# Where a hand-paced attention loop may place the work that runs behind it

## The chip, the cores and the metric

The kernel runs on one core of one Trainium2 chip. The metric is the device time of one execution in microseconds. TensorE, VectorE, ScalarE, GpSimd and the SyncE queue (PE, DVE, ACT, POOL and SP in the profile) each work through their own instructions in order and wait for each other by semaphores; PEld is TensorE's loading of weights.

## The reference

The input is `x` of shape (8, 128, 36, 36), so 8 batch items of N = 1296 positions with 128 channels, in float32. Layer 0 is a convolution with attention; layer 1 is an additive attention over the positions, then a small mixture of experts. Nearly all the time goes to the additive attention, whose score is a sum over 128 channels for each pair of positions:

```python
q = jnp.einsum('bld,ed->ble', x, Wq) + bq
k = jnp.einsum('bld,ed->ble', x, Wk) + bk
t = jnp.tanh(q[:, :, None, :] + k[:, None, :, :])
scores = jnp.einsum('bijd,d->bij', t, w) + bw[0]
attn = jax.nn.softmax(scores, axis=-1)
return jnp.einsum('bij,bjd->bid', attn, x)
```

The kernel does not evaluate the tanh pair by pair. It writes tanh(q + k) as a quotient of sums of exponentials that separate into a part of the query and a part of the key. A matmul of query features `qf` and key features `kf` gives denominators `d`, a second one, with the weighted part of `qf`, gives numerators `n`, and the score is a sum of n/d over groups of channels.

## The kernel before, in words

**The loop.** There are 8 batches, 3 chunks of 432 queries and 11 key tiles, which makes 264 units of (batch, chunk, tile). A unit of a full key tile has 12 slots, k = 0 to 11; the tile with the 16 keys left over (a remainder unit) has 2. That makes 2928 slots, 366 in a batch. In slot p the loop issues, in this order (lines 1031 to 1058):

- `take_turns(p)`: steps of the work behind the loop that need no matmul, such as a VectorE or ScalarE operation that takes the result of a matmul out of PSUM (a "take");
- `numerators(p)` (L903): two matmuls into two banks `n`;
- `denominators(p + LAG)`, LAG = 3 (L886): two matmuls into two banks `d`, for the slot three ahead, and on ScalarE the logarithm of both banks into `lq` (L898) and, in every other slot, the exponential of minus that, four banks at once (L901), so that `lq` holds 1/d;
- `terms(p, ns)` (L908): VectorE multiplies `n` by 1/d;
- `matmul_turn(p)`: at most one group of matmuls of the work behind the loop, which stands on TensorE between d of this slot and n of the next.

**Shapes of the slots.** For k = 0, 1, 3, 4, 6, 7, 9, 10 each matmul contracts 32 rows, on one half of the rows, and n of slot p and d of slot p + 3 use opposite halves. For k = 2, 5, 8, 11 each contracts 64 rows (SLOTS, lines 48 to 53). A float32 matmul shows as two instructions.

**Who sums.** In the 8 slots of a unit that are not in `DVE_PAIRS`, VectorE writes two products to `rp` (L929, two operations) and GpSimd adds them up (L936, L938). In the 4 slots k = 2, 5, 8, 11, VectorE multiplies in place (L923) and adds both banks to `accd` itself (L925), so it has four operations there in place of two; for k = 2 there are three (L918 to L920). At the end of a unit GpSimd joins both sums (L945, L947), and ScalarE takes the exponential of the score (L958).

**Banks.** `ps_d` holds two slots' denominators. `ps_n` is a ring of four banks: two for the numerators of each slot, and each group of the work behind the loop takes one from the same ring. `lq` has three buffers, each for two slots.

**The work behind the loop.** Generators yield before each group of matmuls and before each take. They stand in four lanes (L991), asked in this order: `first_of_all` (features of the next queries, scores of the remainder), `urgent` (the weighted sum of the finished chunk, `attend`), `gates` (the gating of the batch before) and `background` (normalization, convolutions, layer 0, tokens and keys of the next batch). A lane's generator says whether it wants matmuls next and how many slots it rests first. Each group adds its columns, plus 20 per matmul, to `behind[0]` (L256); most groups count 148 to 904 such columns.

**The pace.** `balance` gains PACE columns in every slot and loses what was issued; lanes other than `first_of_all` may issue a group only if it is not negative, and it never rises above PACE. Once a group has been issued, `matmul_turn` stops for this slot:

```python
            before = behind[0]
            for lane in lanes:
                while lane.due(p, True) and behind[0] == before:
                    if lane is not first_of_all and balance[0] < 0 or lane is gates and urgent:
                        break
                    lane.run(p)
            balance[0] = min(balance[0] - (behind[0] - before) + PACE, PACE)
```

`take_turns` asks each lane once, in every slot. Key features go to DRAM and are loaded again two units ahead of their use (`prefetch`, SP's queue). Before the loop the first batch is prepared; after it the experts follow.

Of the kernel before, what the change touches and what calls it, by code (L numbers as in the profile page):

```python
# [55 lines left out]
LAG = 3  # L56
SHIFT = 6.5
DVE_PAIRS = (2, 5, 8, 11)
PACE = 365

# [7 lines left out]
def kernel(  # L70
# [55 lines left out]
    with ExitStack() as loop, ExitStack() as score:  # L126
# [127 lines left out]
        behind = [0]  # L254
# [128 lines left out]
        def conv_keys(b):  # L383
            k = convolved["k"] = big_tile("k0")
            for r0, nr in KROWS:
                yield from conv_turns(
                    taps["k"], (r0, nr), 1, grid(k[:, r0 * WV : (r0 + nr) * WV], WV), True
                )
# [246 lines left out]
        def keys(b, tiles):  # L635

            xT = prepared[b][1]
            yield matmuls(1)
            for t in tiles:
                o, n = KT[t]  # L640
                for q0 in (0, NF // 2):
                    some = slice(q0, q0 + NF // 2)
                    pk = aux("pk1").rearrange("p (q t) -> p q t", t=128)
                    for q in range(NF // 2):
                        bmm(pk[:, q, :n], a_k[:, (q0 + q) * 128 : (q0 + q + 1) * 128],
                           xT[:, o : o + n], start=True, stop=True)
                    yield TAKE
                    ks = kstp.tile([128, NF // 2, 128], F32, tag="ks", name="ks")
                    nc.scalar.activation(ks[:, :, :n], pk[:, :, :n], AF.Exp)
                    kd3 = kd[b][t].rearrange("p (q t) -> p q t", t=128)[:, some, :]  # L650
                    if n == REM:

                        for x in range(2):
                            nc.gpsimd.tensor_scalar(
                                ks[:, :, (x + 1) * n : (x + 2) * n], ks[:, :, :n],
                                pairs[:, min(q0, 1), x : x + 1], None, ALU.mult,
                            )
                        nc.sync.dma_start(kd3[:, :, : 2 * n], ks[:, :, n : 3 * n])
                    else:
                        nc.sync.dma_start(kd3, ks)  # L660
                    if q0 > 0:
                        made.add((b, t))
                    yield matmuls()
# [58 lines left out]
        def gating(b):  # L722
            yield from gate_logits(b, range(NCH))
            yield from gate_tokens(b)
# [122 lines left out]
        slots = []  # L847
# [4 lines left out]
        def prefetch(u):  # L852
            if u < len(units):
                b, c, j = units[u]
                assert (b, j) in made
                n = 128 if j < NKT - 1 else 32
                kf = kfp.tile([128, NF, 128], F32, tag="kf", name="kf")
                nc.sync.dma_start(
                    kf[:, :, :n], kd[b][j].rearrange("p (q t) -> p q t", t=128)[:, :, :n]
                )  # L860
                kf_of[u] = kf

        def new_block(b, c, q):
            qf = qfp.tile([128, 2, CH], F32, tag="qf", name="qf")
            qf_of[b, c, q] = qf
            return query_block(b, c, q, qf)
# [19 lines left out]
        def denominators(p):  # L886

            if p >= len(slots):
                return
            u, k = slots[p]  # L890
            d = ps_d.tile([128, 2, 512], F32, tag="d", name="d")
            n = banks(u, k)
            products(u, k, 0, [d[:, h, :] for h in range(n)])
            if k % 2 == 0:
                lq_of[u, k // 2] = lp.tile([128, 4, CH], F32, tag="lq", name="lq")
            lq = lq_of[u, k // 2]
            o = 2 * (k % 2)
            nc.scalar.activation(lq[:, o : o + n, :], d[:, :n, :CH], AF.Ln)  # L898
            if k % 2 == 1:
                some = lq[:, : o + n, :]  # L900
                nc.scalar.activation(some, some, AF.Exp, scale=-1.0)  # L901

        def numerators(p):  # L903
            ns = [ps_n.tile([128, 512], F32, tag="n", name="n") for _ in range(banks(*slots[p]))]
            products(*slots[p], 1, ns)
            return [ps[:, :CH] for ps in ns]

        def terms(p, ns):  # L908

            u, k = slots[p]  # L910
            lq = lq_of[u, k // 2]
            o = 2 * (k % 2)
            mult = nc.vector.tensor_mul
            rem = units[u][2] == NKT - 1
            if k in DVE_PAIRS and not rem:
                if k == DVE_PAIRS[0]:
                    live["d"] = acc.tile([128, CH], F32, tag="accd", name="accd")
                    mult(live["d"], ns[0], lq[:, o, :])  # L918
                    mult(ns[1], ns[1], lq[:, o + 1, :])
                    nc.vector.tensor_add(live["d"], ns[1], live["d"])  # L920
                else:
                    for h in range(2):
                        mult(ns[h], ns[h], lq[:, o + h, :])  # L923
                    for h in range(2):
                        nc.vector.tensor_add(live["d"], ns[h], live["d"])  # L925
            else:
                rp = rpp.tile([128, 2, CH], F32, tag="rp", name="rp")
                for h, n in enumerate(ns):
                    mult(rp[:, h, :], n, lq[:, o + h, :])  # L929
                if rem:  # L930
                    live.setdefault("rem", []).extend(rp[:, h, :] for h in range(len(ns)))
                elif k == 0:
                    live["r"] = rp
                elif k == 1:
                    live["p"] = acc.tile([128, 2, CH], F32, tag="accp", name="accp")
                    nc.gpsimd.tensor_add(live["p"], live["r"], rp)  # L936
                else:
                    nc.gpsimd.tensor_add(live["p"], live["p"], rp)  # L938
            if k % 2 == 1:
                lq_of.pop((u, k // 2))  # L940
# [50 lines left out]
        first_of_all, urgent, gates, background = lanes = [Lane() for _ in range(4)]  # L991
        balance = [0]

        def take_turns(p):
            for lane in lanes:
                if lane.due(p, False):
                    lane.run(p)

        def matmul_turn(p):


            before = behind[0]
            for lane in lanes:
                while lane.due(p, True) and behind[0] == before:
                    if lane is not first_of_all and balance[0] < 0 or lane is gates and urgent:
                        break
                    lane.run(p)
            balance[0] = min(balance[0] - (behind[0] - before) + PACE, PACE)

        load_x(1)  # L1010
        drain(normal(0))
# [15 lines left out]
        for p, (u, k) in enumerate(slots):  # L1027
            b, c, j = units[u]
            rem = j == NKT - 1
            if k == 0:  # L1030
                prefetch(u + 2)
                if c == 0 and j == 1:
                    if b > 0:
                        gates.append(gating(b - 1))
                    if b + 1 < NB:
                        background.extend(
                            (normal(b + 1), conv_keys(b + 1), layer0(b + 1), tokens(b + 1),
                             keys(b + 1, range(NKT)))
                        )
            take_turns(p)  # L1040
            ns = numerators(p)
            denominators(p + LAG)
            terms(p, ns)
            if pending and pending[0][0] <= p:
                exps(p, *pending.popleft()[1:])
            last = p + 1 == len(slots) or slots[p + 1][0] != u

            if j == order[-1] and u + 1 < len(units) and k % 3:
                used = IN_TURN.index(SLOTS[k][0]) + 1
                if used < NF:  # L1050
                    first_of_all.append(new_block(*units[u + 1][:2], IN_TURN[used]))
            elif j == order[-2] and last and u + 2 < len(units):
                first_of_all.append(new_block(*units[u + 2][:2], IN_TURN[0]))
            matmul_turn(p)
            if last and rem:
                first_of_all.append(rem_scores(p, u, live.pop("rem")))
            elif last:
                pending.append((p + 7, u, sums(u)))
        while pending:
            exps(p, *pending.popleft()[1:])  # L1060
        take_turns(len(slots))
        assert not first_of_all and not gates and not background
        score.close()

# [41 lines left out]
    gates, res = [], []  # L1106
# [140 lines left out]
```

## Time and profile before

| what | value |
|---|---|
| median of 3 runs | 6183.36 us (6181.84 to 6194.64) |
| the profiled execution | 6189.61 us |
| its span, first to last instruction | 6187.9 us |
| mean granted TensorE clock | 0.979 |
| start of batch 1, 3, 4 and 7 in the loop | 921.5, 2400.0, 3140.6, 5359.5 us |
| last slot starts | 6014.0 us |
| L898, logarithm of two banks on ScalarE | 2928 of 879 ns |
| L901, exponential of four banks on ScalarE | 1464 of 1638 ns |
| L929, L923, L925 on VectorE | 600, 608, 603 ns each |
| L938 on GpSimd | 1440 of 2024 ns |
| matmuls of n and of d, per instruction | 574 and 563 ns |

The profile lists instructions by line, engine and tile: `n<-qf,kf` is a matmul that writes numerators, `pa`, `s`, `pc`, `pk` and the like are banks of the work behind the loop. A wait is named as waiting engine and tile, then the one that released it, with the sum of time, how often, and the longest. Batches and slots are told apart in the timeline by counting the numerator matmuls: four instructions in each slot of a full tile.

### The profile page before, as it was taken

How to read it: one execution, taken by the hardware profiler on the slowest of the kernel's cores; microseconds unless marked ns; L12 is line 12 of the kernel's file. 1: busy time of each engine (PE TensorE's matmuls, PEld its weight loads, DVE VectorE, ACT ScalarE, POOL GpSimd, SP SyncE). 2: the span in 40 equal slices, each digit the busy share in tenths (PEclk: the TensorE clock that was granted, in tenths of full speed). 3: DMA queues.
4: the chain of work that ended last, by engine and by line, in shares of the span. 5: the costliest groups of instructions: out<-in, count | busy, mean ns of one | idle time of the engine just before them, and what ended most of it. 6: DMA issues, size and time to landing. Idle time of an engine off the chain costs nothing.

```text
span 6187.9 us, 93159 instructions
## 1 busy us (share of the span) xinstructions
PE 5946.4 (96%) x33576; PEld 2834.5 (46%) x33576; DVE 4799.7 (78%) x9525; ACT 5275.0 (85%) x5371; POOL 4584.2 (74%) x2794
## 2 busy tenths in 40 slices
PE   7999999999999999999999999999999999999996
PEld 5454444544544445444445444454444444544443
DVE  3687778877788787877887777887778878788872
ACT  1798998988989888889988899898998988999980
POOL 3677877777778777778777786877777777787870
PEclk9999999999999999999999999999999999999997
DMA  1210011000110002100111001110011000100017
GB/s 43 70 36 22 21 68 38 33 26 28 67 39 24 26 30 69 37 24 23 50 48 38 22 24 63 41 36 22 21 65 41 31 25 28 63 31 28 25 55 276
DMA packets 150383, 271.40 MB, mean 44 GB/s; under 512 B 45408, under 2 KB 74976, under 8 KB 149920
## 3 DMA queue, kind: packets, MB, share of 16 engines
q1 hardware_dynamic: 149920, 265.44, 12.8%
q8 instruction: 265, 4.34, 0.3%
q14 instruction: 198, 1.62, 0.1%
HBM read 200.94 MB, written 64.19 MB: 43 GB/s over the span
## 4 chain that ended last, share of the span: by engine, by line
PE 65%; DVE 11%; POOL 8%; ACT 8%; issue 8%; DMA 1%; SPq 0%; POOLq 0%; DVEq 0%; ACTq 0%
PE n L875 30%; PE d L875 10%; PE pa L258 7%; ACT lq L898 5%; PE pc L258 5%; DVE n L923 4%; POOL accp L938 4%; DVE rp L929 3%; PE s L258 3%; PE pk L258 3%; DVE accd L925 2%; POOL qf L673 1%; POOL accp L936 1%; PE d L880 1%; PE pq L258 1%
## 5 line engine op out<-in xcount | busy, mean ns | idle before, releaser
L938 POOL TENSOR_TENSOR accp<-accp,rp 128x864 f32<-128x864 f32 x1440 | 2915.1, 2024 | 996.5 <-DVE rp L929 943.5
L875 PE MATMUL n<-qf,kf 32*128 32x432 f32 (+1 forms) x11520 | 3283.6, 574 | 58.9 <-DVE accd L925 19.1
L898 ACT ACTIVATE lq<-d 128x864 f32<-128x864 f32 x2928 | 2517.6, 879 | 555.8 <-PE d L875 498.0
L875 PE MATMUL d<-qf,kf 32*128 32x432 f32 (+1 forms) x11520 | 2907.7, 563 | 46.4 <-ACT lq L898 40.5
L929 DVE TENSOR_TENSOR rp<-n,lq 128x432 f32<-128x432 f32 x3912 | 2160.8, 600 | 557.9 <-PE d L875 398.8
L901 ACT ACTIVATE lq<-lq 128x1728 f32<-128x1728 f32 (+1 forms) x1464 | 2398.2, 1638 | 46.3
L875 PEld LDWEIGHTS n<-qf,kf 32*128 32x128 f32 (+1 forms) x11520 | 1185.9, 185 | 1588.2 <-DVE rp L929 469.1
L875 PEld LDWEIGHTS d<-qf,kf 32*128 32x128 f32 (+1 forms) x11520 | 1046.9, 186 | 449.8 <-issue 241.7
L923 DVE TENSOR_TENSOR n<-n,lq 128x432 f32<-128x432 f32 x1440 | 812.0, 608 | 251.8 <-PE n L875 195.2
L925 DVE TENSOR_TENSOR accd<-n,accd 128x432 f32<-128x432 f32 x1440 | 868.1, 603 | 24.7
L936 POOL TENSOR_TENSOR accp<-rp 128x864 f32<-128x864 f32 x240 | 485.2, 2022 | 244.8 <-DVE rp L929 244.7
L673 POOL TENSOR_SCALAR qf<-qf,cs_s 128x432 f32<-128x432 f32 x192 | 260.7, 1364 | 47.0 <-ACT qf L672 47.0
L258 PEld LDWEIGHTS pa<-xh,e 128*108 128x108 f32 x1920 | 222.1, 174 | 142.9 <-DVE rp L929 63.3
L947 POOL TENSOR_TENSOR accd<-accp,accd 128x432 f32<-128x432 f32 x240 | 265.3, 1106 | 23.3 <-DVE accd L925 3.0
L258 PE MATMUL pa<-xh,e 128*108 128x129 f32 x1920 | 261.3, 283 | 19.9 <-DVE accd L925 13.9
L945 POOL TENSOR_TENSOR accp<-accp 128x432 f32<-128x432 f32 x240 | 264.7, 1103 | 15.8
L258 PE MATMUL s<-q,k 128*116 128x432 f32 x480 | 230.3, 568 | 4.2 <-DVE accd L925 2.7
L444 ACT ACTIVATE e<-s 116x432 f32<-116x432 f32 x240 | 124.8, 520 | 118.7 <-PE s L258 118.4
L258 PEld LDWEIGHTS pk<-xT,a_k 128*128 128x128 f32 x1408 | 171.6, 193 | 105.9 <-DVE n L923 31.8
L435 POOL TENSOR_TENSOR tot<-tot,e 116x432 f32<-116x432 f32 x192 | 212.1, 1105 | 7.3 <-ACT e L444 4.5
L918 DVE TENSOR_TENSOR accd<-n,lq 128x432 f32<-128x432 f32 x240 | 145.1, 604 | 86.7 <-PE n L875 49.7
L258 PE MATMUL pa<-e,vw 116*128 116x432 f32 x480 | 204.6, 549 | 0.0
(208 smaller groups left out, 3870.2 us busy)
## 6 DMA issues: line engine op xcount, KB each, us to landing
kf<-kd SPq DMA_DIRECT2D x240, 512.0 KB
kd<-ks SPq DMA_DIRECT2D x160, 256.0 KB
w<-in_weight_dram SPq DMA_DIRECT2D x32, 1024.0 KB
wk_t<-wk_t_d SPq DMA_DIRECT2D x7, 768.0 KB
wv_t<-wv_t_d SPq DMA_DIRECT2D x7, 768.0 KB
wq_t<-wq_t_d SPq DMA_DIRECT2D x7, 768.0 KB
x<-in_x_dram SPq DMA_DIRECT2D x8, 648.0 KB
t<-tokd SPq DMA_DIRECT2D x96, 54.0 KB
```

Source lines behind the costliest of these rows:

```text
L258: mm(out, lhsT, rhs, **kw)
L673: nc.gpsimd.tensor_scalar(qf[:, 1, :], qf[:, 0, :], cs_s[:, q : q + 1], None, ALU.mult)
L875: mm(outs[h][:, :CH], kf[rows[h], q, :], qf_of[b, c, q][rows[h], part, :], start=True, stop=True)
L898: nc.scalar.activation(lq[:, o : o + n, :], d[:, :n, :CH], AF.Ln)
L901: nc.scalar.activation(some, some, AF.Exp, scale=-1.0)
L923: mult(ns[h], ns[h], lq[:, o + h, :])
L925: nc.vector.tensor_add(live["d"], ns[h], live["d"])
L929: mult(rp[:, h, :], n, lq[:, o + h, :])
L936: nc.gpsimd.tensor_add(live["p"], live["r"], rp)
L938: nc.gpsimd.tensor_add(live["p"], live["p"], rp)
L945: nc.gpsimd.tensor_add(s[:, 0, :], s[:, 0, :], s[:, 1, :])
L947: nc.gpsimd.tensor_add(d, s[:, 0, :], d)
```

## The change

`take_turns` and `matmul_turn` are told k, the number of the slot in its unit. In slots k = 2, 5, 8, 11 `take_turns` now serves only the lane `first_of_all`. `matmul_turn` now lets the other three lanes issue no group if the next slot is one of these four. PACE rises from 365 to 400 columns, and what is saved up may reach 800 in place of 365. The call after the loop passes k = 0.

```diff
-PACE = 365
+PACE = 400
...
-        def take_turns(p):
+        def take_turns(p, k):
             for lane in lanes:
-                if lane.due(p, False):
+                if lane.due(p, False) and (k not in DVE_PAIRS or lane is first_of_all):
                     lane.run(p)
 
-        def matmul_turn(p):
+        def matmul_turn(p, k):
...
             before = behind[0]
             for lane in lanes:
                 while lane.due(p, True) and behind[0] == before:
-                    if lane is not first_of_all and balance[0] < 0 or lane is gates and urgent:
+                    paced = balance[0] < 0 or k + 1 in DVE_PAIRS
+                    if lane is not first_of_all and paced or lane is gates and urgent:
                         break
                     lane.run(p)
-            balance[0] = min(balance[0] - (behind[0] - before) + PACE, PACE)
+            balance[0] = min(balance[0] - (behind[0] - before) + PACE, 2 * PACE)
...
-            take_turns(p)
+            take_turns(p, k)
...
-            matmul_turn(p)
+            matmul_turn(p, k)
...
-        take_turns(len(slots))
+        take_turns(len(slots), 0)
```

## The prediction

> **What bounds the kernel now.** I read the page's engine shares first, then one batch of the loop beside the last batch, then the waits, then the order of TensorE's matmuls in time.
>
> ```profile
> PE 5946.4 (96%) x33576; PEld 2834.5 (46%) x33576; DVE 4799.7 (78%) x9525; ACT 5275.0 (85%) x5371; POOL 4584.2 (74%) x2794
> ```
>
> TensorE shows 96%, but its records overlap and their ends are modelled, so the 85% of ScalarE is the firmer number. The next view gives the busy time in batch 3 (2400.0 to 3140.6 us) and in the last batch, which has no next batch to prepare: length, then PE, PEld, DVE, ACT, POOL.
>
> ```profile
> 2400.00:3140.60 740.60, 723.42 (x4081) 343.76 (x4081) 594.42 (x1180) 658.12 (x670) 570.38 (x346) 0.99 0.12 37
> 5359.50:6016.00 656.50, 632.33 (x3495) 276.31 (x3496) 544.73 (x1060) 613.62 (x599) 525.15 (x297) 1.00 0.08 27
> ```
>
> A batch has 366 slots. With little work behind the loop a slot takes 656.5/366 = 1.79 us with ScalarE 93% busy; with the full load 740.6/366 = 2.02 us with ScalarE at 89%. VectorE is at 80%, GpSimd at 77%. No engine is full: the loop loses about a tenth to engines that wait for each other in turn.
>
> ```profile
> ACT lq L898 <- PE d L875: 498.0, 616, 5.0
> PEld n L875 <- DVE rp L929: 469.1, 875, 1.3
> PEld n L875 <- DVE accd L925: 259.8, 564, 2.5
> DVE n L923 <- PE n L875: 195.2, 266, 1.4
> PEld d L875 <- ACT lq L898: 158.8, 244, 4.6
> ```
>
> ScalarE waits for the denominators' banks; TensorE's weight loads wait for VectorE, the sums (L925) among them; yet in the very slots that the change protects, VectorE waits for TensorE (L923). The last view tells what a group of matmuls behind the loop costs TensorE (start, length in us, then the instruction):
>
> ```profile
> 2002.70 0.98 PE L258 MATMUL s<-q,k 128*112 128x432 f32 x2
> 2003.61 1.17 PE L875 MATMUL n<-qf,kf 64*128 64x432 f32 x4
> 2004.43 1.07 PE L875 MATMUL d<-qf,kf 64*128 64x432 f32 x4
> 2005.43 1.72 PE L258 MATMUL pa<-e,vw 116*128 116x432 f32 x4
> 2007.08 0.63 PE L875 MATMUL n<-qf,kf 32*128 32x432 f32 x2
> ...
> 2008.33 0.53 PE L875 MATMUL d<-qf,kf 32*128 32x432 f32 x2
> 2008.84 1.14 PE L875 MATMUL n<-qf,kf 64*128 64x432 f32 x3
> ```
>
> A group counted as 452 columns held TensorE 2002.70 to 2003.61, 0.91 us; one counted as 904 held it 2005.43 to 2007.08, 1.65 us. So a counted column is (1.65-0.91)/452 = 1.64 ns, and about 0.17 us per group is fixed. From 2007.08 to 2008.84 two slots of 32-row products, n and d interleaved, took 1.76 us together; the slot with 64-row products before them took 1.82 us without its group (2003.61 to 2005.43).
>
> [...] between equal shapes matmuls start 0.36 us apart, but from the last matmul of `pa` (2006.63) to the 32-row ones (2007.08) it is 0.45 us. [...]
>
> **The change part by part.** Call slots class 0 (k = 0, 3, 6, 9), class 1 (k = 1, 4, 7, 10) and class 2 (k = 2, 5, 8, 11, VectorE's own sums). No instruction is added or removed: both programs hold 1480 groups and 870,012 counted columns inside the loop. Counted in the order of the two built programs over the loop's slots, groups stand behind class 0, 1 and 2 slots 455, 492 and 518 times before, and 630, 118 and 725 times after (the 118 are query features, which the rule exempts). Work that "keeps off" the sums loses the turn ahead of a class 2 slot, which is the one behind class 1; the turn inside the class 2 slot itself stays and is used more. Takes and steps at the start of class 2 slots fall from 548 to 118. No bank is held longer: what stands behind class 2 or class 0 is taken in the next slot, as before, so no new wait arises.
>
> *Takes off the sums.* In batches 1 to 6, leaving out slots beside a remainder tile, 222 of 702 class 2 slots have a VectorE take ahead of their terms (0.75 us on average). There the first term starts 0.25 us after its bank is done by the record; with a group before but no VectorE take, -0.06 us. So a take delays the sums by 0.31 us: 222 x 0.31 = 69 us, x7/6 for seven batches = 80 us. That is the most this part brings. But VectorE stood idle 0.24 us just ahead of those terms even with the take, waiting for TensorE, so the take lies mostly beside the group's own matmuls. Its lower bound is nothing.
>
> *Groups moved.* Since the group moves with its take, I price them together by what slots cost now: the distance between the first numerator matmuls of neighbouring slots in the timeline, by class, by whether a group stands behind the slot, and by whether one stood ahead of it (batches 1 to 6, 2106 slots away from remainder tiles).
>
> | class | group behind / ahead | slots before | median us | slots after |
> |---|---|---|---|---|
> | 0 | no / no | 109 | 1.07 | 44 |
> | 0 | no / yes | 228 | 0.84 | 143 |
> | 0 | yes / no | 180 | 2.33 | 84 |
> | 0 | yes / yes | 185 | 2.23 | 431 |
> | 1 | no / no | 109 | 1.27 | 169 |
> | 1 | no / yes | 209 | 0.94 | 461 |
> | 1 | yes / no | 228 | 2.36 | 18 |
> | 1 | yes / yes | 156 | 2.03 | 54 |
> | 2 | no / no | 108 | 1.65 | 109 |
> | 2 | no / yes | 180 | 1.65 | 18 |
> | 2 | yes / no | 192 | 3.02 | 503 |
> | 2 | yes / yes | 222 | 2.74 | 72 |
>
> Counts times medians give 3991.5 us before and 4048.8 after, +57.3. The rows' mean group sizes times the counts after make 24,600 columns too many (711,000 against 686,000), at 1.64 ns 40 us. Left: +17 us, x7/6 = **+20 us**. The reason is visible: behind class 1 a group sits where the tile shape changes anyway (32 to 64 rows) and costs 1.09 to 1.09 us more than none; behind class 0 it splits the two 32-row slots, and costs 1.26 to 1.39; behind class 2, 1.09 to 1.37. With means in place of medians (3.23 for the 192-slot row) the same sum is 4240.4 to 4372.7, +132 - 40 = +92, x7/6 = +107 us: the upper bound.
>
> *PACE 400, allowance up to 800.* It changes when work runs, not how much. The skipped turns eat most of it: the background of a batch ends in slot 2 of the next batch before, in slot 3 after. But the spread is less even: in twelfths of a batch the groups' columns per slot run from 157 to 429, from 216 to 383 before. Three units in which the next query features are made carry 9, 10 and 9 groups before, 10, 11 and 11 after, 4 more or 2.7 thousand columns; at 1.64 ns and the fixed part 2.7 x 1.64 + 4 x 0.17 = 5.1 us. Half of it should come back where those groups left, since lighter stretches are set by ScalarE: 2.5 x 7 = **+17 us** (0 to 36).
>
> *Steps and DMAs.* A moved step carries its loads and stores on SP's queue and its GpSimd operations with it, by one or two slots, 2 to 4 us. Feature loads are issued two units ahead, some 48 us, so a store of keys one slot later is hidden; without that cover each late tile would stop TensorE by about a slot. I cost it at nothing, and the last batch, whose slots ScalarE sets, too. Prologue and tail keep their order.
>
> *Sum.* +20 + 17 = +37 us on the profiled execution's 6189.6 (span 6187.9), that is 6226; this execution lay 6 us over the median of 6183.4, so the forecast is **6220 us**, 0.6% slower.
>
> **Rivals.** *VectorE relief decides (faster).* If the 80 us all reach TensorE through the two banks that class 0 slots take over from the sums, the time is 6183 - 80 = 6103. For it: 259.8 us of weight loads waiting on L925. Against: the idle VectorE ahead of the sums. It decides if over 37 of the 80 us get through, as then they outweigh my +37; all of it less my cost would be 6140.
> *Crowding (much slower).* The mean row prices hold, since long sums with a group behind and a group behind the next slot feed each other: +107 us, 6290. For it: class 2 slots of 3.23 us on average; against: those means hold a few slots of nearly 9 us whose cause is GpSimd or VectorE work at one place in the batch.
> *Nothing happens.* The turn inside the class 2 slot stays, so the slots are not freed at all for TensorE, and shares move about under the same waits: 6183.
>
> **Chances.** Forecast with its neighbours 35%, crowding 12%, nothing 15%, relief 38%. A measurement tells about 0.2% (12 us) from no change, so faster 0.38, same 0.15, slower 0.47. The range runs from just below full relief (6095) to just above crowding (6295).
>
> **What would show it.** Right: the VectorE waits of numerator loads on L925 fall, ScalarE's wait on `d` L898 does not, class 2 slots take about 3 us and class 0 about 2.25; DVE L923 waits longer for TensorE. Wrong: if ScalarE's wait of 498 us falls by more than 40, the relief was real; if the rows of my table shift (class 2 with a group well under 3.0 us), prices taken from the old order do not carry over.

## The result and the profile after

The changed kernel takes 6181.47 us in the median of 20 runs (6175.5 to 6191.09). The kernel before, run beside it, takes 6193.57 us in the median of 20. The ratio is 0.9982, with a 95% interval of 0.9975 to 0.9989: 0.18% faster, where 0.6% slower was forecast. The profiled execution took 6176.24 us, with a span of 6174.6 us.

The page's engine shares, the same view as before:

```profile
PE 5978.4 (97%) x33576; PEld 2873.2 (47%) x33576; DVE 4800.7 (78%) x9525; ACT 5279.7 (86%) x5371; POOL 4584.2 (74%) x2794
```

All engines run as many instructions as before; TensorE is busy 32 us longer in a shorter span. Busy time by stretch, batch 3 and the last batch (length, then PE, PEld, DVE, ACT, POOL):

```profile
2402.40:3139.00 736.60, 726.42 (x4082) 348.29 (x4081) 594.13 (x1180) 658.89 (x670) 570.32 (x346) 0.99 0.12 37
5344.80:6000.80 656.00, 634.44 (x3504) 281.66 (x3504) 544.74 (x1060) 613.83 (x600) 524.38 (x296) 0.99 0.09 28
```

Batch 3 is 4.0 us shorter, the last batch only 0.5. From one batch's first slot to the next's, batches 1 to 6 together are 23.6 us shorter, batch 0 is 11.7 longer (why, I did not trace), and what lies before and behind the loop differs by 3 us or less. So the question is about a full-load batch.

The waits that answer to those shown of before:

```profile
PEld n L875 <- DVE rp L929: 582.1, 1040, 1.6
DVE rp L929 <- PE d L875: 548.1, 769, 18.1
ACT lq L898 <- PE d L875: 511.3, 664, 5.3
...
PEld n L875 <- DVE accd L925: 200.2, 476, 1.3
...
PEld d L875 <- ACT lq L898: 151.1, 206, 5.0
...
DVE n L923 <- PE n L875: 85.5, 107, 2.0
```

Waits for the sums (L925) fell by 60 us, and the longest of them from 2.5 to 1.3 us. That longest wait turned out to be the better clue. Waits for L929 rose by 113 us instead, and ScalarE's by 13. The order of TensorE's matmuls in time (start and length in us):

```profile
2001.81 1.72 PE L258 MATMUL pa<-e,vw 116*128 116x432 f32 x4
2003.45 0.63 PE L875 MATMUL n<-qf,kf 32*128 32x432 f32 x2
...
2004.39 1.00 PE L875 MATMUL n<-qf,kf 64*128 64x432 f32 x4
2005.22 0.89 PE L875 MATMUL d<-qf,kf 64*128 64x432 f32 x4
2006.04 0.98 PE L258 MATMUL s<-q,k 128*116 128x432 f32 x2
2006.95 0.63 PE L875 MATMUL n<-qf,kf 32*128 32x432 f32 x2
```

The 64-row products now have no group ahead of them and one behind. A group costs TensorE what it did: 1.64 us for `pa` (2001.81 to 2003.45), 0.91 us for `s`.

**Where in a batch the time went.** I cut each batch into its 33 units (0 to 32, in order of time) at the first numerator matmul of each, and took the mean difference to before over batches 1 to 6 (us per batch). The runs in the lower rows are told below; the last two keep the order of before and of the change.

| kernel | units 2, 3 | 4, 5 | 24 to 26 | 29 | the other 25 | all |
|---|---|---|---|---|---|---|
| the change | -4.4 | -4.5 | -2.2 | -3.2 | +10.4 | -3.9 |
| turn rule alone, spread as evenly (e7) | -1.6 | -1.7 | +0.3 | -3.2 | +10.7 | +4.4 |
| both rules on class 0 (e8) | -2.1 | -1.5 | -1.7 | -3.4 | +15.2 | +6.5 |
| both rules on class 1 (e6) | -4.3 | -2.5 | -1.7 | -1.6 | +12.9 | +2.8 |
| before, one stall removed (e19) | -3.6 | 0.0 | +0.1 | 0.0 | -1.4 | -4.9 |
| the change, the same stall removed (e20) | -4.7 | -4.5 | -1.7 | -3.2 | +10.7 | -3.4 |

The change is 14.3 us per batch shorter at four places and 10.4 longer over the other 25 units. That alone is no gain or loss at a place, because groups have moved between units as well. Here are the columns of the groups in these units, and in brackets the number of groups, less those of before (per batch, counted in the order of the built programs):

| kernel | units 2, 3 | 4, 5 | 24 to 26 | 29 | the other 25 |
|---|---|---|---|---|---|
| the change | -1644 (-4) | -1640 (-1) | -1649 (-3) | -2220 (-3) | +7054 (+10.8) |
| turn rule alone, spread as evenly (e7) | -2088 (-4) | -36 (+1) | -1197 (-2) | -2220 (-3) | +5344 (+7.7) |

At the prediction's 1.64 ns a column and 0.17 us a group, the change's four places are 13.6 us lighter and the other units 13.4 us heavier: an estimate, but most of the split is load that moved. Unit 29 shows it in the trace; the matmuls of L258 in that unit of batch 3, before and then in the change (length, PE, PEld):

```profile
3042.01:3065.96 23.95, 5.72 (x40) 4.84 (x40) 1.00 0.23 75
3041.10:3061.80 20.70, 1.09 (x8) 0.97 (x8) 1.00 0.10 31
```

So the runs have to tell what is left besides the load. The cleanest are the last two rows, which keep every group in its slot.

### The profile page after: what moved, and what is told of

Read it like the earlier page. It is cut to its first block, busy times and chain, and to the rows that moved or that the text cites. A ratio compares the mean times of both kernels' runs of the same rounds, so it can differ in the third digit from the quotient of the medians.

```text
span 6174.6 us, 93223 instructions
## 1 busy us (share of the span) xinstructions
PE 5978.4 (97%) x33576; PEld 2873.2 (47%) x33576; DVE 4800.7 (78%) x9525; ACT 5279.7 (86%) x5371; POOL 4584.2 (74%) x2794
## 4 chain that ended last, share of the span: by engine, by line
PE 77%; ACT 8%; DVE 6%; issue 6%; POOL 2%; DMA 1%; SPq 0%; POOLq 0%; DVEq 0%; ACTq 0%
PE n L875 37%; PE d L875 12%; PE pa L258 7%; ACT lq L898 5%; PE pc L258 5%; PE s L258 3%; PE pk L258 3%; PE pq L258 3%; DVE rp L929 2%; DVE n L923 1%; DVE accd L925 1%; PE d L880 1%; ACT lq L901 1%; PE n L880 1%; ACT e L958 1%
## 5 line engine op out<-in xcount | busy, mean ns | idle before, releaser
L938 POOL TENSOR_TENSOR accp<-accp,rp 128x864 f32<-128x864 f32 x1440 | 2915.7, 2025 | 1033.8 <-DVE rp L929 938.5
L875 PE MATMUL n<-qf,kf 32*128 32x432 f32 (+1 forms) x11520 | 3323.2, 573 | 46.2 <-ACT e L958 13.3
L875 PE MATMUL d<-qf,kf 32*128 32x432 f32 (+1 forms) x11520 | 2988.8, 561 | 43.5 <-ACT lq L898 38.7
L898 ACT ACTIVATE lq<-d 128x864 f32<-128x864 f32 x2928 | 2523.4, 878 | 538.9 <-PE d L875 511.3
L929 DVE TENSOR_TENSOR rp<-n,lq 128x432 f32<-128x432 f32 x3912 | 2173.7, 600 | 748.2 <-PE d L875 548.1
L901 ACT ACTIVATE lq<-lq 128x1728 f32<-128x1728 f32 (+1 forms) x1464 | 2398.2, 1638 | 46.3
L875 PEld LDWEIGHTS n<-qf,kf 32*128 32x128 f32 (+1 forms) x11520 | 1209.5, 184 | 1602.2 <-DVE rp L929 582.1
L875 PEld LDWEIGHTS d<-qf,kf 32*128 32x128 f32 (+1 forms) x11520 | 1090.9, 185 | 426.2 <-issue 225.2
L923 DVE TENSOR_TENSOR n<-n,lq 128x432 f32<-128x432 f32 x1440 | 815.1, 608 | 138.9 <-PE n L875 85.5
L925 DVE TENSOR_TENSOR accd<-n,accd 128x432 f32<-128x432 f32 x1440 | 867.3, 602 | 24.6
L258 PEld LDWEIGHTS pa<-xh,e 128*108 128x108 f32 x1920 | 223.8, 175 | 123.9 <-DVE rp L929 53.7
L947 POOL TENSOR_TENSOR accd<-accp,accd 128x432 f32<-128x432 f32 x240 | 265.2, 1105 | 18.8
L258 PE MATMUL pa<-xh,e 128*108 128x129 f32 x1920 | 263.1, 284 | 6.0 <-DVE accd L925 3.1
L258 PE MATMUL s<-q,k 128*116 128x432 f32 x480 | 230.4, 568 | 1.7 <-DVE q L290 1.4
L258 PEld LDWEIGHTS pk<-xT,a_k 128*128 128x128 f32 x1408 | 170.3, 191 | 106.4 <-DVE accd L925 33.2
L258 PE MATMUL pa<-e,vw 116*128 116x432 f32 x480 | 204.6, 549 | 0.0
L258 PE MATMUL pk<-xT,a_k 128*128 128x128 f32 (+1 forms) x1408 | 201.4, 286 | 0.1
```

Source lines behind the costliest of these rows:

```text
L258: mm(out, lhsT, rhs, **kw)
L875: mm(outs[h][:, :CH], kf[rows[h], q, :], qf_of[b, c, q][rows[h], part, :], start=True, stop=True)
L947: nc.gpsimd.tensor_add(d, s[:, 0, :], d)
```

## The experiments

Each run's ratio is to the kernel before on the same chip, five rounds, with its 95% interval. Three theories stood at first. RELIEF: takes off the sums free VectorE there, about 0.3 us each. THIN: the gain sits in the first six units of a batch, where normalization and gating crowd each other and the rule on takes spreads their steps. SHAPE: a group's price depends on which of TensorE's shapes it stands between. FILL came after the first four runs: what counts is how long the background lasts in its batch; ended early, the rest of the batch runs light, and the loaded part is denser. The background of a batch ends in slot 2 of the next before, in slot 3 with the change.

**One rule at a time, at the same PACE.** The first keeps the turn rule, the second neither rule (edits to the changed kernel):

```diff
-                if lane.due(p, False) and (k not in DVE_PAIRS or lane is first_of_all):
+                if lane.due(p, False):
```

> The matmul rule and PACE 400 without the rule on takes. Groups stand as in the changed kernel (618, 118, 724 behind classes 0, 1, 2), and the steps at class 2 slots fall from 548 to 166 by that alone. Theory RELIEF (the sums of VectorE gain wherever takes are kept off them): nearly all of the change's gain stays, 0.997 to 0.999 of before. Theory THIN (the gain sits in the first six units of a batch, where normalization and gating load VectorE at once and the rule on takes spreads their steps): it is lost, 1.001 to 1.004. Theory SHAPE (it matters only where a group splits slots of one matmul shape): as the changed kernel, 0.998.

```diff
-                if lane.due(p, False) and (k not in DVE_PAIRS or lane is first_of_all):
+                if lane.due(p, False):
...
-                    paced = balance[0] < 0 or k + 1 in DVE_PAIRS
+                    paced = balance[0] < 0
```

> PACE 400 with up to 800 saved, no rule on slots. RELIEF: no gain, 1.000 to 1.003, since 582 steps stay at class 2 slots. THIN: slower, 1.003 to 1.008, as the unit that gating and normalization share gets 11 groups in place of 9 and the end of a batch runs empty. SHAPE: 1.000, since classes hold what they held.

Measured: 1.0102 [1.0088, 1.0116] and 1.0109 [1.0094, 1.0124]. Both lie outside every range that was expected. Both end the background early, in slots 347 and 323 of 366, so they mix rule and fill, and by themselves they don't tell the one from the other.

**The rules on other slots.** Both rules on class 0 (the diff), and both on class 1, that is k in (1, 4, 7, 10), at PACE 420. They end the background in slot 354, and in slot 22 of the next batch:

```diff
-                if lane.due(p, False) and (k not in DVE_PAIRS or lane is first_of_all):
+                if lane.due(p, False) and (k not in (0, 3, 6, 9) or lane is first_of_all):
...
-                    paced = balance[0] < 0 or k + 1 in DVE_PAIRS
+                    paced = balance[0] < 0 or (k + 1) % 12 in (0, 3, 6, 9)
```

> The same rule and pace laid on the wrong slots: steps are kept off class 0, groups off the turn ahead of it, so groups stand behind classes 0 and 1 (700, 651) and 715 steps fall on class 2. RELIEF: slower than before by 0.5 to 1.5%. THIN: about the changed kernel, 0.996 to 1.001, since the steps are spread as thinly. SHAPE: slower, 1.005 to 1.01, since 700 groups split the pair of 32-row slots (450 before).

> The same rule laid on class 1 with PACE 420: no group splits the pair of 32-row slots (7 behind class 0, 757 behind class 1, 701 behind class 2), while 846 steps fall on class 2, the sums. RELIEF: slower than before by 1% or more. THIN: about the changed kernel, 0.996 to 1.001. SHAPE, by the row prices of the prediction: faster than the changed kernel, 0.990 to 0.995.

Measured: 1.0147 [1.0133, 1.016] and 1.0059 [1.0046, 1.0072]. The first is where RELIEF had it (0.5 to 1.5% slower), the second where no theory had it. In the class 1 run almost no group splits a pair of 32-row slots, which SHAPE calls cheapest, and it is slower than before, though 846 steps at the sums go with it. The change itself has more such splits than before (630 in place of 455), so SHAPE can't be what made it faster.

**Rules at matched fill.** PACE chosen so that the background ends in slot 366 to 371: the turn rule alone (385, first edit above), both rules on class 0 (390), no rule (355):

> The matmul rule alone again, with PACE 385, so that the background ends 371 slots after a batch's start (368 in the kernel before, 369 in the changed one, 347 with PACE 400). Theory FILL (the time follows how evenly the work fills its batch, the slots matter little): as the changed kernel, 0.997 to 1.001. THIN (the rule on takes is what spreads the first units' steps): 1.002 to 1.005. RELIEF: 0.998, as 169 of 548 steps stay at the sums.

> The rules on class 0 in place of class 2, PACE 390, background ending after 369 slots (354 with PACE 400, which took 1.0147). FILL: most of the loss goes, 1.000 to 1.005. RELIEF: it stays, 1.010 or more, since 731 steps lie at the sums. THIN: 1.000 to 1.004.

> No rule on slots; up to two turns' columns may be saved, PACE 355, background ending after 368 slots as before. FILL: 0.999 to 1.002. A theory that the doubled savings themselves crowd groups together: 1.004 to 1.008.

Measured: 1.0076 [1.0064, 1.0089], 1.0104 [1.009, 1.0118] and 0.9998 [0.999, 1.0006]. Only the third is as FILL had it; the first is above every range, and the second is where RELIEF had it (1.010 or more). PACE and the allowance of two PACE cost nothing by themselves once the fill is right, so fill explains the second run of the first pair. The turn rule costs 0.76%, 47 us. From there to the change, the take rule brings 0.94%, some 58 us. Yet only 51 more steps leave the class 2 slots (169 to 118 over the whole loop), since the turn rule has moved the others: 51 x 0.31 us is 16 us. RELIEF as an average is over three times too small for that.

**The change with its background ended early** (PACE 440, slot 336):

> The changed kernel with PACE 440: same rules on the same slots, but the background ends after 336 slots. FILL: 1.006 to 1.012. RELIEF and THIN: 0.998 to 1.002, since no work comes back to the sums and the first units keep their rules.

Measured: 1.0044 [1.0032, 1.0057], between the ranges of the theories. So 0.6% lies in fill alone, with both rules kept.

**The take rule without the turn rule** (PACE 370):

```diff
-                    paced = balance[0] < 0 or k + 1 in DVE_PAIRS
+                    paced = balance[0] < 0
```

> The rule on takes without the rule on groups, PACE 370, up to two turns' columns saved, background ending after 366 slots. Steps at class 2 slots fall from 548 to 118, the same as in the changed kernel, but 419 groups wait two slots for their take in place of one and hold their bank of the ring that long. RELIEF: 0.988 to 0.993, as the turn rule (which alone took 1.0076) is gone. THIN: 0.992 to 0.998. A theory that a held bank stops TensorE more than the take would have cost: 1.003 or more.

Measured: 1.0406 [1.0393, 1.0419]. Groups issued behind class 1 now keep their `n` bank until the sums' slot has passed (419 takes). ScalarE's wait on `d` grows from 498.0 to 715.8 us. Each rule alone loses. With the turn rule beside it, the take rule holds no bank longer.

**The take rule in part of a batch.** Between the turn rule alone and the change, 7.1 of 8.3 us per batch lie in the first six units. The three runs are: before with the take rule there (78 takes held one slot longer), the change with it lifted there (PACE 385), and the change with it only there; the edit of the third is

```diff
-                if lane.due(p, False) and (k not in DVE_PAIRS or lane is first_of_all):
+                if lane.due(p, False) and (k not in DVE_PAIRS or lane is first_of_all or slots[min(p, len(slots) - 1)][0] % 33 > 5):
```

> The kernel before with the rule on takes in the first six units of each batch alone; no rule on groups, PACE 365, background ending after 369 slots. Steps at class 2 fall only from 548 to 485. THIN: 0.991 to 0.996, the gain without the cost of the turn rule. RELIEF: 0.999 to 1.000. FILL: 0.999 to 1.001.

> The changed kernel with the rule on takes lifted in the first six units of each batch, the rule on groups everywhere; PACE 385, so that the background ends after 371 slots. Steps at class 2: 145 in place of 118. THIN: as the turn rule alone, 1.005 to 1.009. RELIEF and FILL: 0.998 to 1.001.

> The complement of the last-but-one run: the changed kernel with the rule on takes in the first six units of a batch alone, the rule on groups everywhere, PACE 400, background ending after 366 slots. THIN: as the changed kernel, 0.997 to 1.000. If the takes of the later units carry part of the gain: 1.002 to 1.006.

Measured: 1.0072 [1.006, 1.0084], 1.0075 [1.0063, 1.0087] and 1.0053 [1.004, 1.0066]. The first is outside every range; the second equals the turn rule alone, as THIN had it: all of the rule's gain went with six of 33 units. The third is 7.9 us per batch faster than before in those units, much like the change (8.8), but loses 11.8 elsewhere, where the change loses 4.9. An edit at one place shifts all later work of its batch, so a part of the rule is not a part of its effect.

**GpSimd's load in those units.** Normalization makes windows of the image there on GpSimd (L371 to L375). In THIN's terms it crowds GpSimd, and the change spreads it. Longer rests between its steps, in before (2 and 3 slots, PACE 380; 4 and 4, PACE 390) and in the change (2 and 3), then a kernel that leaves these operations out for every batch but the first:

```diff
                 eng.tensor_add(u[:, 1], o0, e1)
-                yield step()
+                yield step(2)
                 eng.tensor_sub(u[:, 2], e1, o0)
                 eng.tensor_sub(u[:, 3], o1, o0)
-                yield matmuls(1)
+                yield matmuls(3)
```

> The kernel before, no rule of the change, but the normalization of the next batch rests two slots in place of one after its first GpSimd pair and three in place of one after the second, so that it ends in slot 74 in place of 56 of the batch; PACE 380, background ending after 366 slots. 602 steps stand at class 2, more than the 548 before. THIN: 0.993 to 0.998. RELIEF: 1.000 to 1.004. FILL: 1.000.

> The kernel before with the normalization of the next batch resting four slots after each of its GpSimd pairs, ending in slot 82 (74 when it rested two and three, 56 before); PACE 390, background ending after 366 slots; no rule of the change. THIN: 0.993 to 0.997, the same gain or a little more. If the gain of 0.9959 was chance of one arrangement: 0.999 to 1.004.

> The changed kernel with the normalization thinned as well (rests of two and three slots, ending in slot 74), PACE 400, background ending after 369 slots. If the rule on takes gains by that thinning and by nothing else, the two gains don't add, and what is left of the change is the cost of the rule on groups: 1.000 to 1.004. If the rules gain by themselves: 0.992 to 0.995, the product.

> The kernel before, with its schedule slot for slot, but without the twelve GpSimd subtractions and additions per batch that build the window differences of the next batch (all batches but the first; their convolutions read old values). They take 6.5 us of the one unit, the fifth, in which GpSimd is busy 25.3 of 25.6 us. If the crowded GpSimd sets that unit: it shortens by 2 to 3.5 us, 0.995 to 0.997. If it is VectorE's steps or the groups that set it: 0.999 to 1.000.

Measured: 0.9959 [0.9947, 0.9971], 1.0021 [1.0011, 1.0032], 0.9976 [0.9966, 0.9987] and 0.9992 [0.9984, 1.0]. The first is faster than both kernels, but not by THIN: more rest is slower again, and with the windows gone units 4 and 5 take what they took (0.0 us difference). THIN falls. The first run's units 4 and 5 are 4.2 us per batch shorter, but they also hold 4 groups and 2832 columns fewer, 5.3 us at the prediction's prices. The third is no faster than the change beyond its interval, so the two gains don't add. Why the first run is faster as a whole I did not settle.

**What stood in unit 2.** The timeline of before, batch 3, one-column operations of the normalization and what follows (start, length, operation):

```profile
2460.80 4.11 POOL L938 TENSOR_TENSOR accp<-accp,rp 128x864 f32<-128x864 f32 x2 [2.00 <-DVE rp L929]
2462.12 0.15 DVE L336 COPY gm<-pm 128x1 f32<-128x1 f32 x1
2462.30 0.54 DVE L338 TENSOR_TENSOR dev<-gn_mv,gm 128x1 f32<-128x1 f32 x1
2462.88 2.05 DVE L339 SCALAR_TENSOR_TENSOR dev<-dev,gn_mv 128x1 f32<-128x1 f32 x1
2464.86 1.12 DVE L923 TENSOR_TENSOR n<-n,lq 128x432 f32<-128x432 f32 x2
2465.89 1.23 DVE L925 TENSOR_TENSOR accd<-n,accd 128x432 f32<-128x432 f32 x2
```

L339 computes one number per partition and takes 2.05 us. It does so beside the second of the two L938 additions of GpSimd, whose length it takes on (2.02 us on average): both run from 2462.9 to 2464.9. For the first two batches, where no addition of GpSimd runs beside it, it takes 0.22. It stands right ahead of the four operations of the sums, in a slot the rule protects. The operands differ: L338 and L339 have two inputs in SBUF, and L338 too ends with an addition of GpSimd (0.54 us here, 0.16 in the first batch with none beside it). L336 has its input in PSUM and takes 0.15 beside the first addition; L923, L925 and L929 have one of their two in PSUM and keep their 0.60 us beside the same additions, and none of their 6792 executions took over 0.62. Why their lengths go together with the additions', the traces do not show. TensorE in the same stretch:

```profile
2463.74 0.99 PE L875 MATMUL n<-qf,kf 32*128 32x432 f32 x2
2466.53 0.62 PE L875 MATMUL n<-qf,kf 32*128 32x432 f32 x1 [1.80 <-DVE accd L925]
...
2468.29 1.11 PE L875 MATMUL n<-qf,kf 32*128 32x432 f32 x2
...
2474.48 0.66 PE L875 MATMUL n<-qf,kf 32*128 32x432 f32 x2
```

It stands idle 1.80 us until the sums give back a bank. Soon after, matmuls take 1.1 us in place of 0.63 each, until about 2474. Busy time by stretch; the number behind POOL's is the granted clock:

```profile
2464.00:2467.40 3.40, 1.60 (x8) 0.44 (x7) 3.37 (x7) 2.03 (x2) 0.92 (x1) 1.00 0.00 0
2467.40:2474.23 6.83, 6.83 (x26) 2.70 (x23) 5.07 (x12) 3.42 (x3) 4.67 (x3) 0.50 0.10 35
```

So the blocked operation is followed by two losses here: the 1.80 us of idle time, then 6.8 us at a granted clock of 0.50. Whether the idle time halved it is a question to which I come back below.

In the change the take lies one unit later, in slot 1 and ahead of products, and L339 takes 0.96 us, the rest of a shorter addition of GpSimd (L947) that began just before it. Batch 3, then L339 over all batches (shortest, median, longest in ns) in the change:

```profile
2475.87 1.10 POOL L947 TENSOR_TENSOR accd<-accp,accd 128x432 f32<-128x432 f32 x1
2476.02 0.96 DVE L339 SCALAR_TENSOR_TENSOR dev<-dev,gn_mv 128x1 f32<-128x1 f32 x1
```

```profile
L339 DVE SCALAR_TENSOR_TENSOR dev<-dev,gn_mv x8: 219/962/973, 22.0 to 4683.1; 128x1 f32<-128x1 f32 x8
```

**The stall alone.** The last two runs keep every slot of the schedule and change only these operands, so that each of the three operations reads one tensor from PSUM and the others as one number per partition; in the kernel before, and in the change:

```diff
-            nc.vector.tensor_copy(gm, pm[:, :1])
+            nc.vector.tensor_scalar(gm, pm[:, :1], mv[:, 0:1], None, ALU.subtract)
...
-            nc.vector.tensor_sub(dev, mv[:, 0:1], gm)
-            nc.vector.scalar_tensor_tensor(dev, dev, dev, mv[:, 1:2], ALU.mult, ALU.add)
+            nc.vector.tensor_scalar(pm[:, :1], pm[:, :1], mv[:, 0:1], None, ALU.subtract)
+            nc.vector.tensor_scalar(dev, pm[:, :1], gm, mv[:, 1:2], ALU.mult, ALU.add)
```

> The kernel before, its schedule kept slot for slot; the three one-column operations of the normalization (L336, L338, L339) read one operand from PSUM instead of two from SBUF. STALL theory (the change gained by moving L339, which takes 2.05 us beside a GpSimd addition, away from the sums, and so also spared the halved clock that follows): L339 takes 0.15 to 0.25 us in every batch, the low-clock stretches in unit 2 of the batches are gone, unit 2 falls by 3 to 4 us per batch, all others stay within 0.5 us, ratio to the kernel before 0.9955 to 0.997. TAKES theory (the average delay of takes behind the sums is what counts): the takes stand where they stood, so unit 2 stays within 1 us of before and the ratio is 0.999 to 1.001.

> The changed kernel with the same edit of L336, L338 and L339. STALL theory: its unit 2 has been relieved already (L339 at 0.96 us), so it gains at most 0.1% against the changed kernel: ratio to the kernel before 0.997 to 0.9985, and it is not faster than the kernel before with the same edit; then the change's gain was this stall alone. TAKES theory: 0.998, but 0.2% faster than the kernel before with the same edit, as the changed kernel is faster than the kernel before.

Measured: 0.9956 [0.9944, 0.9969] and 0.9977 [0.9967, 0.9987]. Batch 3 of the first, and L339 over all its batches:

```profile
2451.66 4.12 POOL L938 TENSOR_TENSOR accp<-accp,rp 128x864 f32<-128x864 f32 x2 [1.99 <-DVE rp L929]
2453.36 0.28 DVE L339 TENSOR_SCALAR dev<-pm,gm,gn_mv 128x1 f32<-128x1 f32 x1
2453.55 1.12 DVE L923 TENSOR_TENSOR n<-n,lq 128x432 f32<-128x432 f32 x2
```

```profile
L339 DVE TENSOR_SCALAR dev<-pm,gm,gn_mv x8: 276/276/280, 22.2 to 4658.6; 128x1 f32<-128x1 f32 x8
```

L339 takes 0.28 us in every batch, beside the same GpSimd additions, and TensorE's 1.80 us of idle time is gone. Unit 2 is 3.7 us shorter per batch, and every other unit within 0.2, but for unit 6 with -1.3. Unit 2 of batches 3 to 5, before and then in this run:

```profile
2446.04:2474.48 28.44, 25.79 (x121) 11.60 (x121) 26.45 (x53) 21.32 (x21) 21.44 (x12) 0.88 0.13 43
3186.67:3215.15 28.48, 25.83 (x122) 11.69 (x121) 26.47 (x54) 21.36 (x21) 21.54 (x12) 0.88 0.13 44
3927.58:3953.55 25.97, 25.13 (x122) 11.99 (x121) 25.58 (x53) 20.98 (x21) 19.45 (x11) 0.87 0.11 39
```

```profile
2436.91:2460.65 23.74, 22.89 (x122) 11.29 (x121) 23.57 (x53) 20.99 (x21) 19.47 (x11) 1.00 0.13 43
3170.70:3196.68 25.98, 25.14 (x122) 11.61 (x121) 23.95 (x53) 21.01 (x21) 19.46 (x11) 0.87 0.11 40
3907.13:3930.88 23.75, 22.91 (x122) 11.30 (x121) 23.57 (x53) 21.01 (x21) 19.49 (x11) 1.00 0.13 43
```

In unit 2 the full clock came back in five of batches 1 to 6. In batch 4 it did not, and there the unit took 25.98 us: the halved clock is 2.2 us of the 4.7 between 28.4 and 23.7. The clock can fall there without the stall, then, and it did so in the kernel before too: in batches 2 and 5 it fell about 2.5 us ahead of L339. Batch 5 of before, around the fall:

```profile
3938.53:3941.94 3.41, 3.20 (x19) 1.49 (x20) 3.38 (x9) 1.73 (x3) 1.80 (x1) 1.00 0.02 5
3941.94:3948.77 6.83, 6.83 (x24) 3.13 (x23) 6.54 (x12) 4.48 (x5) 4.03 (x2) 0.50 0.09 32
```

TensorE had been busy for 3.20 of 3.41 us when its clock fell. L339 took its 2.05 us there as well, at 3944.4, but TensorE, at half its clock, was never idle, and the unit took 25.97 us, as it does in batch 4 of the new run with nothing blocked. So there a stall beside a halved clock cost nothing, while in the four batches where it came at full clock the unit took 4.3 to 4.9 us more than the 23.7 without it. What halves the clock there I can't explain, and these traces do not tell what makes it fall. Nor is unit 6's -1.3 surely the edit's: it is a half-clock stretch (6.8 us from 2532.2 in batch 3 of before) that comes and goes, and the run without the windows, which keeps the stall, shows the same -1.3.

The stall theory's times are met, but for unit 6; of the low-clock stretches it was right in five batches of six, and L339's 0.28 us is just above its range. That takes would stay worth their average is refuted. In the second run unit 2 is as in the change (24.4 and 24.1 us), so the change had already gained nearly all of this stall. The four kernels together give the cause of the change's gain:

| ratio to before | with the stall | without it |
|---|---|---|
| order of before | 1 | 0.9956 |
| order of the change | 0.9982 | 0.9977 |

Without the stall the order of the change is slower, by 0.9977/0.9956, that is 0.2% or 13 us, though the two intervals just touch. Taking the stall away is worth 0.44%, 27 us, in the order of before and 0.05% in that of the change, which is within the intervals. By these four ratios the change is faster because it moved this one operation away from the sums; that it would be slower without that is less sure than that it would not be faster.

**The other places** were read, not isolated, and the lighter load there explains much of them. Layer 0's tanh (L482, 1.38 us) stands between two loads of function tables on ScalarE (1.28 us each). What stands ahead of it, before and then in the change:

```profile
2982.13 1.64 ACT L901 ACTIVATE lq<-lq 128x1728 f32<-128x1728 f32 x1
2983.79 1.28 ACT L482 ACT_TABLE_LOAD   x1
```

```profile
2972.65 0.87 ACT L898 ACTIVATE lq<-d 128x864 f32<-128x864 f32 x1
2973.54 1.28 ACT L482 ACT_TABLE_LOAD   x1
```

The three take the same 3.94 us in both; but before, the table load begins right after a long L901 and TensorE then idles 3.91 us, while in the change a logarithm (L898) has slipped in ahead and it idles 2.97. The turn rule alone has it at yet another slot, and loses 2.5 us there in unit 25. In unit 4 the gate's exponential (L795, 1.36 us) before lies ahead of the reciprocals for which the sums wait (1.47 us, L923 on L901); in the change it runs four slots later, when they have been served. Of the 3.2 us that unit 4 is shorter, 1.5 are its lighter load at the prediction's prices. The step in unit 29, which the turn rule alone has too, is load: 3 groups and 2220 columns fewer, 4.1 us at those prices, for a measured 3.2.

## Why the prediction was wrong, step by step

*Takes off the sums: costed at nothing. This step failed.* It said that 222 takes delay the sums by 0.31 us each, 80 us at most, and that an idle VectorE (0.24 us on average) hides it. The average was the fault. One of these takes, L336 to L339, held VectorE for 2.7 us ahead of the sums and cost 3.7 us per batch by itself. The operand edit shows it: worth 27 us in the order of before and next to nothing in that of the change, so the move of this one take gave some 24 us, and turned a loss of some 13 us into a gain of 12. An average idle time covers no 2-us operation.

At matched fill the take rule as a whole brings some 58 us from the turn rule alone to the change. How much of that is this stall was not isolated: the turn rule alone has L339 at 1.88 us, and units 2 and 3, where the change has 444 columns more than it, make 2.7 of the 8.3 us per batch. In units 4 and 5 the change has 1604 columns less, which accounts for the 2.8 us there. The rest stays open. The rival "VectorE relief" had its condition met, over 37 of 80 us getting through, but the part of it that is shown came from one blocked operation, not from an average delay.

*Groups moved, +20 us, and PACE, +17.* The direction was right and the size too large: without the stall the order of the change costs 13 us in place of 37. The turn rule alone costs 47 us at matched fill, but it has the stall as well. The unit table can't price this step, since 7054 columns moved into the 25 units that got longer. The crowding of the three query feature units is 4.2 us per batch, where 5.1 had been worked out, half of it to come back. PACE itself costs nothing (0.9998), so long as the background lasts to the batch's end. That condition the working had stated and not priced; it is worth 0.6% (the change at PACE 440) to 1.1% (no rule, 400 against 355).

*The table's rows.* They did not carry over in full. Class 2 with a group behind and none ahead was to stay at 3.02 and came to 2.94 us in the median, its mean fell from 3.23 to 3.00; class 0 between two groups fell from 2.23 to 2.05 (mean from 2.42 to 2.15). The working put the long slots of the first row down to "GpSimd or VectorE work at one place in the batch". They are the slots of layer 0's tanh, on ScalarE, 7.7 to 8.5 us; in the change they stand in class 0 and take 6.4 to 7.5, so most of that row's fall is a move. The stall itself lay in the other row: the slot behind it, class 0 between two groups, took 4.2 to 5.3 us in batches 1, 3, 4 and 6, and 2.0 with the operand edit.

*0.45 us between starts in place of 0.36.* The working set the step from `pa` to the 32-row products against the step between equal shapes. The same stretch has 0.45 us between two matmuls of one shape (`s`, 2002.70 and 2003.15), so the 0.45 us shows no cost of a change of shape. Class 1's lower price (1.09 us for a group) was read from the slots themselves; that it comes from the change of shape was my estimate.

*Steps and DMAs, nothing.* Perhaps wrong for ScalarE's long steps: where the tanh and the gate's exponential fall among the logarithms goes along with 1.8 and 3.2 us in their units, part of it load.

*What would show it.* As foretold: waits on L925 fell, ScalarE's on `d` did not fall, class 2 slots take 3.0 us. Not as foretold: class 0 slots between groups take 2.05 us in place of 2.25, and VectorE's L923 waits less for TensorE (195.2 to 85.5 us), because it is L929, in the other slots, that waits more (398.8 to 548.1).

*Crowding* (6290) did not come: its mean prices contained the tanh's long slots and the stall, which move. Two edits beat both kernels: longer rests in the normalization (0.9959) and the operands in PSUM (0.9956). Both together were not run.

## What to carry to other kernels

Before pricing a moved step by the average of its kind, list the few longest slots and waits of one period and ask which single instruction stands ahead of each; here the reordering was decided by where one of them landed. Where an instruction takes much longer than it does elsewhere (here L339, 2.05 us in place of 0.22) and ends with another engine's, changing an operand's memory may be worth more than a new order (0.9956 in place of 0.9982); an edit that keeps the order is also the clean test. Compare schedules only at equal fill, since a pace that ends its work early can cost as much as the rule under test, and count the load of a stretch before calling its shorter time a gain.

## What the hardware showed that was not expected

A 128x1 operation (L339) took 0.22 us with no GpSimd addition beside it, 0.96 beside the rest of L947 and 2.05 beside L938, 1.88 in the turn rule alone, and 0.28 in every batch with one tensor operand, in PSUM. The granted clock fell to half for 6.8 us after TensorE had been idle for 1.8 us, but also after 3.41 us in which it had been busy for 3.20; beside a clock already halved the same blocked operation cost nothing in the one batch where the two fell together for 6.8 us. The mean granted clock rose from 0.979 to 0.983 in the change (0.021 x 6187.9 - 0.017 x 6174.6 = 25 us less withheld) and to 0.984 with the operand edit in before, yet it was 0.981 for the change with that edit, so a single execution's clock is no measure of what a stall costs.
